# The pair stage's second layer in four column tiles of 32, the gate by Silu, row maxima by accumulation

## The chip, the cores and the metric

The kernel runs on one core of a Trainium2 chip. The metric is the device time of one execution in microseconds. Shapes in profile lines are partitions x elements; "128*32" after a matmul means 128 rows of the array by 32 of its columns.

## The reference

For 4 sequences x[b] of 512 tokens by 512 features, four blocks follow each other, each on a layer norm of the running x and each added to it: a sparse attention, a gated feed-forward, a differential attention, and the same feed-forward again. Cut to what matters here:

```python
h = einsum('bsd,fd->bsf', xn, W1)                       # 128 features
pair = relu(h[:, :, None, :] - h[:, None, :, :] + b1)   # every pair of tokens i, j
pair = relu(einsum('bijf,gf->bijg', pair, W2) + b2)     # second layer, 128 -> 64
sim = einsum('bijg,og->bijo', pair, W3)[..., 0] + b3    # one number for each pair
... # the 51 best j for each i; 32 heads of width 2 attend to these alone
h = silu(gate) * up ; out = h @ w_down                  # feed-forward, 512 -> 2048 -> 512
... 
score = softmax(attn1 - lam * attn2)                    # differential attention, 16 heads
```

The second layer of the pair stage is the largest single piece: 4 x 512 x 512 pairs, each 128 by 64.

## The kernel before

Nothing is issued where it is written. The kernel's functions record every operation as a task with its dependencies (`Plan.add`), and at the end `Plan.issue` plays the tasks through a model of the engines, with costs (`Plan.cost`), buffer counts and due times, several times over, adds a table of fixed offsets for parts of the program (`SHIFT`), and takes the order that the model ends first. The engines then get their instructions in that order, each engine in its own queue, and each queue runs in order. That is why nearly all profile lines carry the one line number L391 (the call in `issue`); the tiles' names tell the work apart. A change of a cost, a rank or an offset can therefore move any instruction of any queue.

The names: f0 to f3 is the first feed-forward of each sequence, e0 to e3 the second, b0 to b3 the differential attention; the pair stage has m, z, r and sim.

**Pair stage** (`pairs`, `pair_group`, `pair_sums`). A group is two values of i against all 512 values of j. VectorE makes m (128 features x 2 x 512) with one `min` for each i; the min form stands for the relu, and the rest is put into the bias `zb`. Each m is read as two f16 halves. TensorE multiplies by `w2s`, the second layer's weights as two f16 parts: three products for each i, into a PSUM tile z of 128 partitions, 64 output features for the first i and 64 for the second. These are matmuls with 64 output columns, so each uses half of the array's columns: column tile 0 for the first i, column tile 1 for the second. The array works on both at once if they are issued one after the other. In 80 of the 1024 groups (`ACT_TILES`) ScalarE makes m instead, in f32, and one f32 product replaces the three. ScalarE then takes z through relu into r. For every 4 groups `pair_sums` adds four matmuls with 32 columns each (four column tiles, f32) into `sim`. There are 7 PSUM buffers of the tag z, 6 of m, 10 of r, 1 of sim.

**Top-k** (`topk_tile`). For each of 16 tiles of 128 rows, VectorE finds the 51 best, GpSimd gathers their keys and values, VectorE and ScalarE (Exp) do the softmax.

**Feed-forward** (`ffn`). For 16 column blocks, 24 full-width f16 matmuls make gate and up (gu[0], gu[1]); the gate is made by ScalarE's Tanh and two VectorE passes; the product goes, as two f16 parts, into the down matmuls.

**Differential attention** (`attn_b`, `stack`). In `stack`, 64 score tiles of each sequence are made once for the softmax's maximum and sum: a VectorE `tensor_reduce` over the tile, a small VectorE product with the scale, ScalarE's Exp with an accumulated sum. Later the transposed scores pass through Exp into pt, and `products` adds four 32-column matmuls, one for each head, into av.

At the end of `hybrid_block`, `weave` puts the pair stage of sequences 1 to 3 (`main`) beside the other blocks of 0 to 2 (`side`); the rest of the blocks of 2 and 3 follow after the pairs.

Of the kernel before, what the change touches and what calls it, by code (L numbers as in the profile page):

```python
# [44 lines left out]
def _size(dt):  # L45
# [7 lines left out]
SHIFT = {  # L53
# [15 lines left out]
}  # L69
# [36 lines left out]
class Plan:  # L106
# [9 lines left out]
    DRAIN = 0.1  # L116
    BUSY = 8.0
    PERIOD = 3.41333
    LAG = {"PE": 0.2, "ACT": 0.135, "DVE": 0.12, "POOL": 0.06, "SP": 0.1}
# [8 lines left out]
    def __init__(self, nc):  # L128
        self.tasks, self.tiles, self.tags = [], {}, {}
        self.behind = ((), 0.0)  # L130
        self.pause = {}
        E = mybir.EngineType
        self.kinds = {"PE": E.PE, "ACT": E.Activation, "DVE": E.DVE, "POOL": E.Pool, "SP": E.SP}
        engs = (("PE", nc.tensor), ("ACT", nc.scalar), ("DVE", nc.vector), ("POOL", nc.gpsimd), ("SP", nc.sync))
        self.engines = [self.Engine(self, k, e) for k, e in engs]
# [57 lines left out]
    @staticmethod  # L193
    def span(ap):

        item = _size(ap.dtype)
        dims = list(ap.ap)
        lo = ap.offset
        if ap.space == DRAM:
            return 0, 1, lo * item, (lo + sum(s * (n - 1) for s, n in dims) + 1) * item  # L200
        p0 = ap.start_partition()
        lo -= p0 * dims[0][0] if lo >= dims[0][0] and dims[0][0] else 0
        return p0, p0 + ap.shape[0], lo * item, (lo + sum(s * (n - 1) for s, n in dims[1:]) + 1) * item

    def add(self, key, eng, op, a, k):
# [137 lines left out]
    def issue(self, tc, rounds=5):  # L343
# [26 lines left out]
        for r in range(rounds + 2):  # L370
# [14 lines left out]
            _, bs, _ = self.run([-e for e in end], before, nsuc, tags, True)  # L385
            rank = [-(bs[i] + tasks[i][7]) for i in range(n)]
        order = best[1]
# [7 lines left out]
def hybrid_block(ctx: ExitStack, tc: tile.TileContext, I, out):  # L395
# [64 lines left out]
    s_gu, s_d, s_a, s_p, s_w = (sc[:, i : i + 1] for i in range(5))  # L460
    c_tanh, c_down, c_exp, c_proj, c_kv, w_up, w_dn, c_nexp = (sc[:, i : i + 1] for i in range(5, 13))
    w2s = const("w2s", [128, 2, 64], F16)
# [64 lines left out]
    def prep_scales():  # L527
# [19 lines left out]
        p = [pw[:, i : i + 1] for i in range(4)]  # L547
        V.tensor_scalar(c_tanh, p[0], 2.0 ** -20, None, ALU.mult)
        V.tensor_scalar(c_down, p[0], p[0], 2.0 ** -16, ALU.mult, ALU.mult)
        V.tensor_scalar(c_down, c_down, p[1], None, ALU.mult)  # L550
# [3 lines left out]
    def prep_lambda():  # L554
# [24 lines left out]
        V.tensor_scalar(c_exp, c_exp, mx, None, ALU.mult)  # L579
        V.tensor_scalar(c_nexp, c_exp, -1.0, None, ALU.mult)  # L580


# [144 lines left out]
    def pair_group(b, it, k, g):  # L727

        hw, zb, _, _, h32, m1 = st_a[b]
        i1 = it * 128 + g * 32 + k  # L730
        m = pp.tile([128, 2, S], F32, name=f"m{b}_{i1}", tag="m", bufs=6)
        z = acct(f"z{b}_{i1}") if b == 0 and g % 2 else pzt(f"z{b}_{i1}")
        r = pp.tile([128, S], F32, name=f"r{b}_{i1}", tag="r", bufs=R_BUFS)
        if (b, it) in ACT_TILES and ACT_STEPS(k, g):

            for s in range(2):
                i = S + i1 + 16 * s
                A.activation(m[:, s, :], h32[:, 0:S], AF.Relu, scale=-1.0, bias=h32[:, i : i + 1])
                mm(z[64 * s : 64 * s + 64, :], h32[:, 2 * S :], m[:, s, :], True, True)
            bias = m1[:, 4:5]  # L740
        else:

            V.tensor_scalar(m[:, 0, :], hw[:, 0, :], hw[:, 1, i1 : i1 + 1], None, ALU.min)
            V.tensor_scalar(m[:, 1, :], hw[:, 0, :], hw[:, 1, i1 + 16 : i1 + 17], None, ALU.min)
            mv = m.bitcast(F16).rearrange("p a (n t) -> p a n t", t=2)
            for n, (w, t) in enumerate(((0, 0), (1, 1), (0, 1))):
                for s in range(2):
                    mm(z[64 * s : 64 * s + 64, :], w2s[:, w, :], mv[:, s, :, t], n == 0, n == 2)
            c = it * 64 + g * 16 + k
            bias = zb[:, c : c + 1]  # L750
        A.activation(r, z, AF.Relu, bias=bias)
        return r

    sims_open = {}

    def pair_sums(b, it, k, rr):
# [5 lines left out]
        for g in range(4):  # L762
            mm(sim[32 * g : 32 * g + 32, :], w3[:, 15 - k : 47 - k], rr[g], k == 0, k == 15)
        if k < 15:
# [132 lines left out]

    def ffn(name, X, first=False, late=False, store=lambda t: None):
        xt = yield from normed_t(name, X)
# [27 lines left out]
        for c in range(NC):  # L927
# [23 lines left out]
            t = fp.tile([128, S], F32, name=f"{name}t{c}", tag="ft", bufs=2)  # L951
            A.activation(t, gu[0], AF.Tanh, scale=c_tanh)
            V.scalar_tensor_tensor(t, t, 1.0, gu[0], ALU.add, ALU.mult)
            V.scalar_tensor_tensor(t, gu[1], 2.0 ** -35, t, ALU.mult, ALU.mult)
            ha, hb = (fp.tile([128, 2, H], F16, name=f"{name}h{p}{c}", tag="fh", bufs=FH) for p in "ab")
# [23 lines left out]
    def attn_b(name, X, first=False, late=False):  # L979
# [54 lines left out]
        def stack(g):  # L1034
# [11 lines left out]
            SP.dma_start(ks[96:98].rearrange("p h n -> p (h n)"), rows_d)  # L1046
            nm = fp.tile([128, 3, 4, 4], F32, name=f"{name}nm{g}", tag="nm", bufs=2)
            for h in range(4):
                for t in range(NT):
                    z = z_(f"{name}s{g}_{h}_{t}")  # L1050
                    mm(z, qs[0:96, h, t * 128 : (t + 1) * 128], ks[0:96, h, :], True, True)
                    V.tensor_reduce(nm[:, 0, h, t : t + 1], z, AX.X, ALU.max)
                    if True:
                        V.tensor_scalar(nm[:, 2, h, t : t + 1], nm[:, 0, h, t : t + 1], c_nexp, None, ALU.mult)
                        A.activation(z, z, AF.Exp, scale=c_exp, bias=nm[:, 2, h, t : t + 1], accum_out=nm[:, 1, h, t : t + 1])
                    yield s_cost
# [5 lines left out]
            nf = nm.rearrange("p a h t -> p (a h t)")  # L1062
            V.tensor_scalar(nf[:, 0:16], nf[:, 0:16], -(2.0 ** -11), None, ALU.mult)
            V.tensor_scalar(nf[:, 16:32], nf[:, 16:32], 2.0 ** -9, None, ALU.mult)
# [18 lines left out]
        def products(o, st, pt, l):  # L1083
            for h in range(4):
                mm(o[32 * h : 32 * h + 32, :], l(h), pt[h], st == 0, st == NT - 1)
            return 0.85

# [3 lines left out]
        for g in range(4):  # L1091
# [4 lines left out]
            for st in range(NT):  # L1096
                pt = [ppool.tile([128, S], F32, name=f"{name}pt{g}_{st}_{h}", tag=ptag, bufs=PT) for h in range(4)]
                for h in range(4):
                    z = z_(f"{name}st{g}_{st}_{h}")
                    mm(z, ks[:, h, st * 128 : (st + 1) * 128], qs[:, h, :], True, True)  # L1100
                    A.activation(pt[h], z, AF.Exp, scale=c_exp)
                    yield s_cost
                    yield next(pre, 0)
# [81 lines left out]
    def f2(b):  # L1185
        def g():
            yield from ffn(f"e{b}", X[b], late=b > 1, store=lambda t: store(b, t))
        return g
# [8 lines left out]
        lambda: start(0),  # L1197
        lambda: weave((f1(0, first=True)(), 1, 0), (phase_a(2), 0.2, 20)),
        at(0, first=True),
        lambda: weave((f2(0)(), 1, 0), (phase_a(3), 0.2, 20)),  # L1200
        lambda: start(1), f1(1), at(1), f2(1), lambda: start(2), f1(2, late=True))
    emit(weave((main, 1, 0), (side, 1.8, 120)))
# [59 lines left out]
```

## Time and profile before

| | |
|---|---|
| time, 3 runs (us) | 2619.89, 2635.37, 2633.38; median 2633.38 |
| the profiled execution's own time (us) | 2631.7 |
| its span (us) | 2629.9 |
| busy (us): TensorE, VectorE, ScalarE, GpSimd | 2556.9, 2067.3, 1516.4, 938.8 |
| matmuls and weight loads in the trace | 15044 each |
| table loads on ScalarE | 1, of 1.283 |
| first and last z of the pair stage (us from the start) | 31.9, 1876.2 |

The span is one execution as the profiler recorded it; busy time counts an instruction from its start to its modelled end, overlaps once. A matmul's duration includes the time until its result stands in PSUM, which overlaps with the next; what a matmul costs in a row is read from the distances of starts.

### The profile page before, as it was taken

The page shows a single profiled execution, that of the slowest core. Times are in us where ns is not written, and L with a number is a line of the kernel's source. Part 1 is how long each engine was busy: PE and PEld are TensorE (multiplying, and loading weights), DVE is VectorE, ACT ScalarE, POOL GpSimd, SP SyncE. Part 2 cuts the span into 40 slices and gives each one's busy share as a digit, 9 for nine tenths or more (in the row PEclk, how much of TensorE's full clock was granted, in tenths as well). Part 3 has the DMA queues.
Part 4 walks back from the last instruction along what each step waited for, and adds up shares of the span by engine and source line. Part 5 has one row for each costly group of instructions (what it writes and reads, how often), then busy time and mean ns, then how long its engine had stood idle before and what let it go on. Part 6 is the DMA issues. An engine that isn't in the chain of part 4 may idle for free.

```text
span 2629.9 us, 42770 instructions
## 1 busy us (share of the span) xinstructions
PE 2556.9 (97%) x15044; PEld 1034.6 (39%) x15044; DVE 2067.3 (79%) x5224; ACT 1516.4 (58%) x2813; POOL 938.8 (36%) x847
## 2 busy tenths in 40 slices
PE   8999999999999999999999999999999999999999
PEld 4334334343333333434433433344444444443444
DVE  8789999989999999888777899987646664574422
ACT  7998888545558984443343489753212476496211
POOL 0367677366741442673434241446143000000000
PEclk9999999999999999999999999999999999999999
DMA  6431311055761113334434421024576534532554
GB/s 203 134 116 55 101 39 51 27 173 168 228 201 38 41 53 104 118 112 149 147 103 132 137 83 41 24 77 135 181 215 193 155 95 135 179 114 89 178 157 151
DMA packets 223628, 317.79 MB, mean 121 GB/s; under 512 B 29969, under 2 KB 150865, under 8 KB 222390
## 3 DMA queue, kind: packets, MB, share of 16 engines
q1 hardware_dynamic: 197302, 261.54, 31.8%
q0 software_dynamic: 26112, 53.53, 7.1%
q8 instruction: 118, 1.93, 0.3%
q14 instruction: 96, 0.79, 0.1%
HBM read 263.43 MB, written 51.39 MB: 120 GB/s over the span
## 4 chain that ended last, share of the span: by engine, by line
PE 72%; DVE 11%; DMA 5%; issue 5%; ACT 4%; POOL 2%; another core or an unknown queue 1%; SPq 1%; DVEq 0%; ACTq 0%; POOLq 0%
PE z L391 20%; PE sim L391 7%; DVE m L391 4%; PE f1z L391 3%; PE e2z L391 3%; PE e1z L391 3%; PE e0z L391 3%; PE f3z L391 3%; PE e3z L391 2%; PE f2z L391 2%; DVE g L391 2%; POOL g L391 2%; ACT r L391 2%; PE f0z L391 1%; ACT wn L391 1%
## 5 line engine op out<-in xcount | busy, mean ns | idle before, releaser
L391 DVE TENSOR_SCALAR m<-hw 128x512 f32<-128x512 f32 x1888 | 819.7, 483 | 74.8 <-PE z L391 52.5
L391 PE MATMUL z<-m,w2s 128*64 128x512 f16 x5664 | 769.3, 393 | 19.5 <-ACT r L391 7.0
L391 ACT ACTIVATE r<-z,zb 128x512 f32<-128x512 f32 x944 | 614.2, 697 | 263.7 <-PE z L391 163.8
L391 POOL DMA_INDIRECT g<-kv,ix x432 | 473.2, 1095 | 431.5 <-DVE ix L391 313.9
L391 POOL DMA_INDIRECT g<-kv,idx x384 | 456.3, 1188 | 357.0 <-DVE idx L391 167.8
L391 PEld LDWEIGHTS <-w2s 128*64 128x64 f16 x5688 | 320.1, 108 | 531.1 <-issue 257.1
L391 PE MATMUL sim<-r,w 128*32 128x512 f32 x2048 | 329.3, 604 | 1.2 <-ACT r L391 0.8
L391 PE MATMUL z<-m,h 128*64 128x512 f32 x320 | 116.8, 599 | 1.4 <-ACT m L391 0.9
L391 ACT ACTIVATE m<-h 128x512 f32<-128x512 f32 x160 | 108.9, 731 | 13.6 <-PE z L391 11.6
L391 POOL TENSOR_SCALAR_AFFINE_SELECT sims<-sims 128x128 f32<-128x128 f32 x16 | 6.0, 378 | 285.8 <-ACT sims L391 285.7
L391 PE MATMUL f3z<-f3xt,f3w 128*128 128x512 f16 x384 | 104.6, 379 | 0.9 <-DVE f3xt L391 0.9
L391 PE MATMUL e2z<-e2xt,e2w 128*128 128x512 f16 x384 | 102.3, 379 | 0.0
L391 PEld LDWEIGHTS sim<-r,w 128*32 128x32 f32 x2048 | 50.4, 108 | 125.1 <-issue 118.5
L391 DVE TENSOR_TENSOR g<-g,sc 128x832 f32<-128x832 f32 (+3 forms) x128 | 97.7, 780 | 0.1
L391 PE MATMUL f0z<-f0xt,f0w 128*128 128x512 f16 x384 | 95.5, 380 | 1.6 <-issue 1.6
L391 PE MATMUL f2z<-f2xt,f2w 128*128 128x512 f16 x384 | 92.8, 384 | 2.2 <-DMA f2w<-wf 2.2
L391 PE MATMUL f1z<-f1xt,f1w 128*128 128x512 f16 x384 | 89.1, 385 | 4.2 <-ACT r L391 2.4
L391 PE MATMUL e3z<-e3xt,e3w 128*128 128x512 f16 x384 | 92.8, 379 | 0.1
L391 PE MATMUL e1z<-e1xt,e1w 128*128 128x512 f16 x384 | 92.6, 382 | 0.0
L391 PE MATMUL e0z<-e0xt,e0w 128*128 128x512 f16 x384 | 87.8, 379 | 0.0
L391 DVE MAX8 vm<-sims 128x8 f32<-128x512 f32 x112 | 76.3, 682 | 3.8 <-issue 2.0
L391 DVE FIND_INDEX8 ix<-vm,sims 128x8 uint32<-128x512 f32 x112 | 76.4, 682 | 0.0
(642 smaller groups left out, 3868.4 us busy)
## 6 DMA issues: line engine op xcount, KB each, us to landing
f0wr<-wf SPq DMA_DIRECT2D x48, 256.0 KB
wn<-wgu SPq DMA_DIRECT2D x32, 256.0 KB
wf<-f0w SPq DMA_DIRECT2D x16, 512.0 KB
e0w<-wf SPq DMA_DIRECT2D x16, 512.0 KB
f1w<-wf SPq DMA_DIRECT2D x16, 512.0 KB
e1w<-wf SPq DMA_DIRECT2D x16, 512.0 KB
f2w<-wf SPq DMA_DIRECT2D x16, 512.0 KB
f3w<-wf SPq DMA_DIRECT2D x16, 512.0 KB
```

The costliest lines, as they stand in the source:

```text
L391: getattr(eng, op)(*a, **k)
```

## The change

Five edits come together.

- In `pair_group` every product goes into four column tiles of 32 (`w_ = 32`): 64 output features as two matmuls of 32 columns, for each of the two i. A group has 12 f16 matmuls for 6 (or 4 f32 for 2), each with its own weight load.
- `Plan` gets `together` and `level`: the matmuls of a group share the earliest rank among them, so the model orders them side by side; and `plan.behind` makes the model treat each of a group's matmuls as ready only when both halves of m are made (for sim: when all four r are; for av: when all four pt are), with fixed pauses READY and MADE in place of the engines' general lag. These two change the order alone; the waits on the chip still follow the data.
- In `ffn`, with `silu=True` (f0, e0, f1, e1 and f2), ScalarE's Silu gives the gate, and one VectorE pass with a scalar from memory (`c_up`) multiplies by up. f3, e2 and e3 keep Tanh.
- In `stack`, one VectorE `tensor_scalar` multiplies the scores by the negative scale in place and accumulates their minimum; Exp then takes the scaled scores with a constant scale of -1. `nm` loses its third plane, and three small scalars (`c_iexp`, `c_gate`, `c_up`) are made once.
- The table `SHIFT` has new values.

```diff
+    READY, MADE = 0.185, 0.17
...
+    def together(self, n):
+        self.groups.append(range(len(self.tasks) - n, len(self.tasks)))
+
+    def level(self, rank):
+        for g in self.groups:
+            r = min(rank[i] for i in g)
+            for i in g:
+                rank[i] = r
+        return rank
...
-            rank = [-(bs[i] + tasks[i][7]) for i in range(n)]
+            rank = self.level([-(bs[i] + tasks[i][7]) for i in range(n)])
...
+        V.tensor_scalar(c_gate, p[0], 2.0 ** -19, None, ALU.mult)
+        V.tensor_scalar(c_up, ipw[:, 0:1], 2.0 ** -15, None, ALU.mult)
...
+        V.reciprocal(c_iexp, c_exp)
+        V.tensor_scalar(c_iexp, c_iexp, 2.0 ** -11, None, ALU.mult)
...
-        i1 = it * 128 + g * 32 + k
+        i1, w_ = it * 128 + g * 32 + k, 32
...
-                mm(z[64 * s : 64 * s + 64, :], h32[:, 2 * S :], m[:, s, :], True, True)
+            made = (len(plan.tasks) - 2, len(plan.tasks) - 1)
+            for s in range(2):
+                for u in range(0, 64, w_):
+                    plan.behind = (made, plan.READY)
+                    mm(z[64 * s + u : 64 * s + u + w_, :], h32[:, 2 * S + u : 2 * S + u + w_], m[:, s, :], True, True)
+            plan.together(128 // w_)
...
+            made = (len(plan.tasks) - 2, len(plan.tasks) - 1)
             for n, (w, t) in enumerate(((0, 0), (1, 1), (0, 1))):
                 for s in range(2):
-                    mm(z[64 * s : 64 * s + 64, :], w2s[:, w, :], mv[:, s, :, t], n == 0, n == 2)
+                    for u in range(0, 64, w_):
+                        plan.behind = (made, plan.MADE)
+                        mm(z[64 * s + u : 64 * s + u + w_, :], w2s[:, w, u : u + w_], mv[:, s, :, t], n == 0, n == 2)
+            plan.together(384 // w_)
...
-        return r
+        return r, len(plan.tasks) - 1
...
-            mm(sim[32 * g : 32 * g + 32, :], w3[:, 15 - k : 47 - k], rr[g], k == 0, k == 15)
+            plan.behind = (tuple(i for _, i in rr), plan.READY)
+            mm(sim[32 * g : 32 * g + 32, :], w3[:, 15 - k : 47 - k], rr[g][0], k == 0, k == 15)
+        plan.together(4)
...
+            if silu:
+                A.activation(t, gu[0], AF.Silu, scale=c_gate)
+                V.scalar_tensor_tensor(t, gu[1], c_up, t, ALU.mult, ALU.mult)
+            else:
+                A.activation(t, gu[0], AF.Tanh, scale=c_tanh)
+                V.scalar_tensor_tensor(t, t, 1.0, gu[0], ALU.add, ALU.mult)
+                V.scalar_tensor_tensor(t, gu[1], 2.0 ** -35, t, ALU.mult, ALU.mult)
...
-                    V.tensor_reduce(nm[:, 0, h, t : t + 1], z, AX.X, ALU.max)
-                    if True:
-                        V.tensor_scalar(nm[:, 2, h, t : t + 1], nm[:, 0, h, t : t + 1], c_nexp, None, ALU.mult)
-                        A.activation(z, z, AF.Exp, scale=c_exp, bias=nm[:, 2, h, t : t + 1], accum_out=nm[:, 1, h, t : t + 1])
+                    V.tensor_scalar(z, z, c_nexp, 3.0e38, ALU.mult, ALU.min, accum_out=nm[:, 0, h, t : t + 1])
+                    A.activation(z, z, AF.Exp, scale=-1.0, bias=nm[:, 0, h, t : t + 1], accum_out=nm[:, 1, h, t : t + 1])
...
-            V.tensor_scalar(nf[:, 0:16], nf[:, 0:16], -(2.0 ** -11), None, ALU.mult)
+            V.tensor_scalar(nf[:, 0:16], nf[:, 0:16], c_iexp, None, ALU.mult)
...
         def products(o, st, pt, l):
             for h in range(4):
+                plan.behind = (pt[4], plan.READY)
                 mm(o[32 * h : 32 * h + 32, :], l(h), pt[h], st == 0, st == NT - 1)
+            plan.together(4)
```

More of the change, by code (lines that the diff above doesn't have):

```diff
@@ L131, in __init__ @@
         self.pause = {}
+        self.groups = []
         E = mybir.EngineType
@@ L460, in hybrid_block @@
     s_gu, s_d, s_a, s_p, s_w = (sc[:, i : i + 1] for i in range(5))
-    c_tanh, c_down, c_exp, c_proj, c_kv, w_up, w_dn, c_nexp = (sc[:, i : i + 1] for i in range(5, 13))
+    c_tanh, c_down, c_exp, c_proj, c_kv, w_up, w_dn, c_nexp, c_gate, c_up, c_iexp = (sc[:, i : i + 1] for i in range(5, 16))
     w2s = const("w2s", [128, 2, 64], F16)
@@ L895, in hybrid_block, with ffn @@
     PARTS = ((0, 0), (0, 1), (1, 0))
-    def ffn(name, X, first=False, late=False, store=lambda t: None):
+    def ffn(name, X, first=False, late=False, silu=False, store=lambda t: None):
         xt = yield from normed_t(name, X)
@@ L951, in ffn @@
             t = fp.tile([128, S], F32, name=f"{name}t{c}", tag="ft", bufs=2)
-            A.activation(t, gu[0], AF.Tanh, scale=c_tanh)
-            V.scalar_tensor_tensor(t, t, 1.0, gu[0], ALU.add, ALU.mult)
-            V.scalar_tensor_tensor(t, gu[1], 2.0 ** -35, t, ALU.mult, ALU.mult)
+            if silu:
[5 more added lines that the diff above has]
+                V.scalar_tensor_tensor(t, gu[1], 2.0 ** -35, t, ALU.mult, ALU.mult)
             ha, hb = (fp.tile([128, 2, H], F16, name=f"{name}h{p}{c}", tag="fh", bufs=FH) for p in "ab")
@@ L1046, in stack @@
             SP.dma_start(ks[96:98].rearrange("p h n -> p (h n)"), rows_d)
-            nm = fp.tile([128, 3, 4, 4], F32, name=f"{name}nm{g}", tag="nm", bufs=2)
+            nm = fp.tile([128, 2, 4, 4], F32, name=f"{name}nm{g}", tag="nm", bufs=2)
             for h in range(4):
@@ L1096, in attn_b @@
             for st in range(NT):
-                pt = [ppool.tile([128, S], F32, name=f"{name}pt{g}_{st}_{h}", tag=ptag, bufs=PT) for h in range(4)]
+                pt = [ppool.tile([128, S], F32, name=f"{name}pt{g}_{st}_{h}", tag=ptag, bufs=PT) for h in range(4)] + [[]]
                 for h in range(4):
@@ L1101, in attn_b @@
                     A.activation(pt[h], z, AF.Exp, scale=c_exp)
+                    pt[4].append(len(plan.tasks) - 1)
                     yield s_cost
@@ L1186, in g @@
         def g():
-            yield from ffn(f"e{b}", X[b], late=b > 1, store=lambda t: store(b, t))
+            yield from ffn(f"e{b}", X[b], late=b > 1, silu=b < 2, store=lambda t: store(b, t))
         return g
@@ L1197, in hybrid_block @@
         lambda: start(0),
-        lambda: weave((f1(0, first=True)(), 1, 0), (phase_a(2), 0.2, 20)),
+        lambda: weave((f1(0, first=True, silu=True)(), 1, 0), (phase_a(2), 0.2, 20)),
         at(0, first=True),
         lambda: weave((f2(0)(), 1, 0), (phase_a(3), 0.2, 20)),
-        lambda: start(1), f1(1), at(1), f2(1), lambda: start(2), f1(2, late=True))
+        lambda: start(1), f1(1, silu=True), at(1), f2(1), lambda: start(2), f1(2, late=True, silu=True))
     emit(weave((main, 1, 0), (side, 1.8, 120)))
```

30 rows, old and new, of the table SHIFT are left out of this document.

## The prediction

> **What bounds the kernel now.** I read the page's head first, then its slices, the costliest groups, TensorE's timeline in the pair stage, the chain of waits, and last the waits of TensorE.
>
> ```profile
> span 2629.9 us, 42770 instructions
> PE 2556.9 (97%) x15044; PEld 1034.6 (39%) x15044; DVE 2067.3 (79%) x5224; ACT 1516.4 (58%) x2813; POOL 938.8 (36%) x847
> ...
> PE   8999999999999999999999999999999999999999
> ...
> DVE  8789999989999999888777899987646664574422
> ACT  7998888545558984443343489753212476496211
> ...
> PEclk9999999999999999999999999999999999999999
> ```
>
> TensorE is busy in every slice and its clock is full, so the time is TensorE's instructions plus what holds them apart. VectorE is nearly as full in the first half; it is second in line.
>
> ```profile
> L391 DVE TENSOR_SCALAR m<-hw 128x512 f32<-128x512 f32 x1888 | 819.7, 483 | 74.8 <-PE z L391 52.5
> L391 PE MATMUL z<-m,w2s 128*64 128x512 f16 x5664 | 769.3, 393 | 19.5 <-ACT r L391 7.0
> L391 ACT ACTIVATE r<-z,zb 128x512 f32<-128x512 f32 x944 | 614.2, 697 | 263.7 <-PE z L391 163.8
> ...
> L391 PE MATMUL sim<-r,w 128*32 128x512 f32 x2048 | 329.3, 604 | 1.2 <-ACT r L391 0.8
> ```
>
> VectorE's "m" and ScalarE's "r" mostly wait for TensorE's z, hardly the reverse. A matmul's 393 ns is latency, not its cost. The timeline prices it (columns: start, length, then the instructions):
>
> ```profile
> 100.34 2.42 PE L391 MATMUL z<-m,w2s 128*64 128x512 f16 x18
> ...
> 104.65 0.87 PE L391 MATMUL z<-m,w2s 128*64 128x512 f16 x6 [0.79 <-DVE m L391]
> 105.45 1.06 PE L391 MATMUL sim<-r,w 128*32 128x512 f32 x8
> 106.44 0.42 PE L391 MATMUL z<-m,w2s 128*64 128x512 f16 x2
> ```
>
> Eighteen z matmuls are nine rounds of two, side by side in the two column tiles: (2.42 - 0.39 for the last one's latency) / 9 = 0.226 us a round. Six matmuls from 104.65 are three rounds and would let the next begin at 105.33; "sim", four tiles of 32, begins at 105.45, and its own two f32 passes of 0.432 us (single starts in the trace) would end at 106.31, but z begins at 106.44. So each change of tile width costs 0.09 to 0.13 us; I take 0.09, the single starts' value (0.316 where a round is 0.226). Full-width matmuls come from the chain of waits:
>
> ```profile
> 2549.17 15.54 PE e3z L391 x72
> ```
>
> 15.54 / 72 = 0.216 us each.
>
> With these prices (0.216 full, 0.226 a narrow round, 0.432 an f32 pass, 0.09 a width change) I went once through TensorE's instructions in the order built before, each matmul starting when its own column tile is free and those ahead of it have started. That adds up to 2496 us, of which 88 are 980 width changes. The profiled execution took 2631.7 us (span 2629.9; the median of the runs is 2633.4, 0.1% more), so 136 us are waits for data, start and end. That rest grows evenly: 39 us by the first feed-forward block (at 500 us), 71 by 1020, 112 by 1890.
>
> **The change, part by part.** The same order, read from the changed program, gives these terms.
>
> 1. Width changes. z, sim and the attention's "av" now share width 32: 546 changes for 980. 434 x 0.09 = 39 us less, all on TensorE's path.
>
> 2. Half-empty rounds. Without the width changes the old order sums to 2407 us, the new one to 2379: 29 less. Most of it (20) is the 80 groups whose m ScalarE makes: each half was issued alone when its own m was there, now all four tiles are ordered together once both are. The z rounds give 10, sim and av nearly nothing. A group's first matmul now waits for the later half of m, and behind it TensorE's whole queue; the planner puts the group later by as much, and the seven z buffers hide it, unless r comes late.
>
> 3. Four tiles in a round. Arithmetic per z is unchanged: three rounds of four instead of three of two, 944 x 3 = 2832 rounds. But every round issues four weight loads and four matmuls for two and two. No row shows f16 in four tiles. Nearest below: the full-width 0.216, 0.010 under a pair's round. Above: the most matmuls that the trace starts in any 5 us are 46, 9.2 per us; at that rate four would take 0.435 us, +592 in all. Nearest by far is sim: four loads and four matmuls start 7 ns apart, and a column's next pass comes on time 0.432 us later. The last of four starts 21 ns after the first against 3 in a pair, mostly hidden in the next round. I take 0.230: +11. Bounds: -28 and +592.
>
> [...]
>
> 4. Silu. In f0, e0, f1, e1 and f2 (80 column blocks) the gate needs one VectorE pass fewer.
>
> ```profile
> L391 DVE SCALAR_TENSOR_TENSOR f0t<-f0z,f0t 128x512 f32<-128x512 f32 x16 | 10.9, 678 | 6.0 <-remote 5.8 <-PE f0z L391 0.2
> L391 DVE SCALAR_TENSOR_TENSOR f0t<-f0t,f0z 128x512 f32<-128x512 f32 x16 | 10.8, 678 | 1.9 <-ACT f0t L391 1.7 <-issue 0.2
> ...
> L391 DVE SCALAR_TENSOR_TENSOR X<-f0a,sc,X 128x512 f32<-128x512 f32 x2 | 1.4, 734 | 0.0
> L391 ACT ACT_TABLE_LOAD x1 | 1.3, 1283 | 0.8 <-PEq L1255 0.8
> ```
>
> Two passes of 678 ns become one with a scalar from memory, 734 by the X row: 0.62 us less, 50 us of VectorE in all. On the path only what TensorE waits for it counts:
>
> ```profile
> PE aop L391 <- DVE e1t L391: 4.7, 1, 4.7
> PE z L391 <- DVE f0t L391: 4.1, 2, 2.4
> ```
>
> With e0t's 1.3 that is 10 us; I take half, -5 (bounds 0 and -10). But the changed program has 23 table loads for 1: Silu and Exp alternate wherever a top-k's softmax or the attention meets a gate. 22 x 1.283 = 28 us on ScalarE, and behind each load the r that sim waits for. ScalarE is idle 42% of the time and ten r buffers stand between, so I let about a third through: +10 (bounds 0 and +28).
>
> [...]
>
> 5. Maxima. 256 times
>
> ```profile
> L391 DVE TENSOR_REDUCE b2nm<-b2s 128x1 f32<-128x512 f32 x64 | 43.5, 687 | 35.1 <-PE b2s L391 34.8
> L391 DVE TENSOR_SCALAR b2nm<-b2nm,sc 128x1 f32<-128x1 f32 x64 | 12.8, 210 | 1.0
> ```
>
> become one pass over the scores that also accumulates. Not in the trace; bounds 537 ns (xs, 128x512 in SBUF) and 810 (xnT, out of PSUM, two scalars). By the PSUM rows I take 0.75: 0.15 us less each, 38 of VectorE. The Exp after it loses its scale pointer. VectorE waits here for TensorE (34.8 of 35.1), so on the path: nothing (bounds -5, +5). If that cover went, the 38 us would be the price.
>
> 6. Everything moves: the planner gets new offsets, so every queue is reordered, SP's 1025 and POOL's 816 transfers too, none added. For the rest of 136 us I know no better value than itself; if it shrank to the idle time the page shows (2631.7 - 2556.9 = 75) it would give 61, and I keep 30 either way.
>
> Sum: 2631.7 - 39 - 29 + 11 - 5 + 10 = 2580, 2% faster. About 1% is what a measurement of this kernel can tell from no change.
>
> **The rivals.**
>
> Slower: the round of four is bound by issue. The gain of terms 1, 2 and 4 is 63 us; it is gone once a round passes 0.226 + 63 / 2832 = 0.248. At 0.270, a fifth of the way from a pair's round to the 0.435 of term 3, 2631.7 - 63 + 2832 x 0.044 = 2693. For it: twice the rate of matmuls that the trace ever holds. Against: sim's starts. Chance 0.12.
>
> No change: VectorE takes over. Up to the first feed-forward block the new order asks 412 us of TensorE; VectorE's work there, by starts (m every 0.396 us, not 0.483), is 398, where before it was 461 against 412. The two then run level, and each jitter counts. If the 49 us of that stretch are lost but for 10, and the rest stays, 2580 + 39 = 2619. For it: nines in VectorE's slices 4 to 7. Against: m's idle time ends with TensorE's z. Chance 0.14.
>
> More than forecast: order and shorter chains also thin out the waits, -30: 2550; it is inside my own case.
>
> **How the numbers follow.** Forecast 0.74, no change 0.14, slower 0.12. Low end: rounds at 0.216 (39 less than I take) and 10 from the waits: 2580 - 49, so 2531. High end: the no-change case at 2619 with all the table loads (+18) and a little of the slow round: 2645. Faster by over 1% means under 2607: 0.74; within: 0.14; slower: 0.12.
>
> **What would show it.** Right: z rounds of four start 0.226 to 0.235 us apart; TensorE's busy time falls by about 60 us; its waits stay near 75; the first feed-forward block starts near 460 us, not 500. Wrong: rounds over 0.245; "m" as the main releaser of TensorE's z before 460 us; waits of PE z for r just after table loads summing to over 30 us. A span above 2620 with rounds of 0.23 would mean that the rest of 136 us grew, term 6.

## The result: slower by 4.65%, and on another chip no change

| | before | after | ratio, 95% interval |
|---|---|---|---|
| first measurement, median of 6 runs each (us) | 2628.71 | 2746.97 | 1.0465 [1.0439, 1.0491] |
| profiled execution (us) | 2631.7 | 2746.6 | |

The forecast was 2580. The head of the page of after, some of its costliest groups, and what TensorE waited for (us in all, times, longest):

```profile
span 2744.8 us, 54646 instructions
PE 2590.4 (94%) x21028; PEld 1155.9 (42%) x21028; DVE 2014.4 (73%) x5148; ACT 1525.9 (56%) x2835; POOL 930.2 (34%) x847
...
PE   8999899789999999999999999999989899999999
...
DVE  8779988879989999678775879988455455584432
```

```profile
L403 PE MATMUL z<-m,w2s 128*32 128x512 f16 x11328 | 908.2, 396 | 63.1 <-issue 34.6
L403 DVE TENSOR_SCALAR m<-hw 128x512 f32<-128x512 f32 x1888 | 818.2, 485 | 195.0 <-PE z L403 106.9
```

```profile
PE z L403 <- issue: 35.6, 63, 1.5
PE sim L403 <- ACT r L403: 16.6, 17, 3.6
PE z L403 <- DVE m L403: 15.8, 16, 2.8
```

TensorE has 21028 matmuls for 15044, and gaps that before hardly has. VectorE, which was nearly full, is less full than before and waits for z. The longest "wait" of z is no wait: "issue" is idle time in which TensorE waited for nothing that the profile shows. One such place in TensorE's timeline (start, length, instructions, idle time before):

```profile
1925.75 1.56 PE L403 MATMUL z<-m,w2s 128*32 128x512 f16 x24
1928.18 0.42 PE L403 MATMUL z<-m,w2s 128*32 128x512 f16 x2 [0.87 <-issue]
1929.62 0.42 PE L403 MATMUL z<-m,w2s 128*32 128x512 f16 x2 [1.02 <-issue]
1931.04 1.33 PE L403 MATMUL z<-m,w2s 128*32 128x512 f16 x4 [1.00 <-issue]
1933.86 1.31 PE L403 MATMUL z<-m,w2s 128*32 128x512 f16 x4 [1.49 <-issue]
```

Twenty-four matmuls in 1.56 us, then two, two, four and four with about a microsecond between. In the single starts such a place reads load, 0.70 us, matmul, a load and a matmul at once, 0.71 us, load, 0.71 us, matmul. Call it a pause when a TensorE record (a load or a matmul) that waits for no semaphore starts 0.58 us or more after the record before it. By this count after has 86 pauses, 67 us in all, 63 of them between 0.66 and 0.74 us; before has one. (The expectations below speak of 80, by a narrower count.)

### The profile page after: what moved, and what is told of

It reads as the page before. It is cut to its first block, busy times and chain, and to the rows that moved or that the text cites. A ratio compares the mean times of both kernels' runs of the same rounds, so it can differ in the third digit from the quotient of the medians.

```text
span 2744.8 us, 54646 instructions
## 1 busy us (share of the span) xinstructions
PE 2590.4 (94%) x21028; PEld 1155.9 (42%) x21028; DVE 2014.4 (73%) x5148; ACT 1525.9 (56%) x2835; POOL 930.2 (34%) x847
## 4 chain that ended last, share of the span: by engine, by line
PE 68%; DVE 14%; ACT 5%; DMA 4%; issue 4%; POOL 2%; another core or an unknown queue 1%; SPq 0%; DVEq 0%; ACTq 0%; POOLq 0%
PE z L403 19%; PE sim L403 7%; DVE m L403 5%; PE e1z L403 3%; PE e2z L403 3%; PE f1z L403 3%; PE f3z L403 3%; PE f2z L403 3%; ACT r L403 3%; PE e0z L403 3%; DVE g L403 2%; PE e3z L403 2%; POOL g L403 2%; PE b1qk L403 1%
## 5 line engine op out<-in xcount | busy, mean ns | idle before, releaser
L403 PE MATMUL z<-m,w2s 128*32 128x512 f16 x11328 | 908.2, 396 | 63.1 <-issue 34.6
L403 POOL DMA_INDIRECT g<-kv,ix x432 | 482.5, 1117 | 466.8 <-DVE ix L403 259.5
L403 PEld LDWEIGHTS <-w2s 128*32 128x32 f16 (+1 forms) x11352 | 412.6, 95 | 491.1 <-issue 243.1
L403 POOL DMA_INDIRECT g<-kv,idx x384 | 437.3, 1139 | 458.0 <-DVE idx L403 276.3
L403 PE MATMUL sim<-r,w 128*32 128x512 f32 x2048 | 398.9, 598 | 19.7 <-ACT r L403 16.6
L403 PEld LDWEIGHTS sim<-r,w 128*32 128x32 f32 x2048 | 105.5, 108 | 132.9 <-ACT r L403 60.0
L403 PE MATMUL z<-m,h 128*32 128x512 f32 x640 | 129.6, 595 | 5.5 <-ACT m L403 3.7
L403 PE MATMUL e0z<-e0xt,e0w 128*128 128x512 f16 x384 | 95.6, 380 | 3.5 <-ACT r L403 1.9
L403 PE MATMUL e1z<-e1xt,e1w 128*128 128x512 f16 x384 | 98.3, 385 | 0.0
```

The source lines that it names most:

```text
L403: getattr(eng, op)(*a, **k)
```

## The experiments

Each set ran on one chip, the kernel before beside the rest; the chip's number is known for all but the first measurement. The times and the pauses turned out to differ between chips; chip 13 was met in one set only, and the first measurement's chip could be the same one, so whether the chip or its state at that time makes the difference is not shown. "A chip with pauses" is short for either.

**First set, chip 7: the narrow tiles alone, the wide tiles in the new order, Tanh for Silu, twice the instructions without narrow tiles.** Before took 2585.2 us here. In x1 and x4 the planned order of before is kept, and a product is split only as it is given to the engine.

```diff
 x1: before, each z matmul as two of 32 columns
+ for u in (0, 32):  z[64*s+u : 64*s+u+32, :], w2s[:, w, u:u+32], mv[:, s, :, t]
 x2: after's order, each pair of 32-column matmuls as one of 64
+ if u == 0:         z[64*s : 64*s+64, :],     w2s[:, w, :],      mv[:, s, :, t]
 x3: after
-                A.activation(t, gu[0], AF.Silu, scale=c_gate)
+                A.activation(t, gu[0], AF.Tanh, scale=c_gate)
 x4: before, each f16 z matmul as two halves of j
+ for v in (0, 256): z[64*s : 64*s+64, v:v+256], w2s[:, w, :], mv[:, s, v:v+256, t]
```

x3 computes another gate; the work is the same, without table loads.

> The kernel before, same order of all queues, but each 64-column z matmul is issued as two of 32 columns one after the other (the planner does not know). By the prices of before the order sums to 2457 us on TensorE (2496 before), so with the old rest of 136 us: 2593. Theory A, TensorE runs out of instructions when twice as many are issued (the 0.70 us pauses without a semaphore, 80 of them in the trace after): pauses like those appear, 60 us or more, and the time is 2640 to 2700. Theory B, the new order and its pauses are at fault: no pauses, about 2593. Theory C, the table loads: about 2593.

> The changed kernel in its own order of all queues, but each two 32-column z matmuls of one half are issued as one of 64 columns at the place of the first. The order was not made for that: it has 1189 width changes and sums to 2589 us on TensorE (2428 as it was). Theory A (instruction supply): the 0.70 us pauses are gone, and the rest over the sum falls from 319 us to 150 to 230, so 2740 to 2820. Theory B (order): the rest stays at 319 or more, 2900 and over. Theory C (table loads): the rest falls by nothing either, 2900.

> The changed kernel with Tanh in Silu's place, all else and every queue's order kept: the gate's value is wrong, and the 22 additional table loads are gone. Theory C (table loads): 2747 falls to 2690 or less. Theories A and B: the loads' own 28 us at most, a third of it by the forecast, so 2725 to 2745.

> The kernel before in its own order, two column tiles of 64, but each f16 z matmul of 512 columns is issued as two of 256 with a weight load each, alternating between the two column tiles: as many TensorE instructions as after the change, the same array time (the order sums to 2502 us, 2496 before), no four tiles. Theory A (instruction supply): pauses of 0.70 us without a semaphore, and 2690 to 2760. Theory D, four column tiles are slow in themselves: 2630 to 2645, no pauses. Theories B and C: the same 2630 to 2645.

| | us | ratio to before there | pauses |
|---|---|---|---|
| x1, narrow tiles alone | 2565.8 | 0.9938 [0.9916, 0.9961] | 0 |
| x2, new order in wide tiles | 2717.5 | 1.0520 [1.0499, 1.0542] | 1 |
| x3, Tanh for Silu | 2581.2 | 0.9993 [0.9980, 1.0006] | 2 |
| x4, instructions doubled, wide tiles | 2598.7 | 1.0051 [1.0033, 1.0069] | 0 |

None of these has the changed kernel's pauses. x2 is slow for another reason: the new order with two tiles has 1189 width changes and adds up to 2589 us. The times expected for x1, x2 and x4 all missed: they were worked out from the first measurement, and before itself took some 45 us less here. x3 fell where theory C had it, as if Silu's tables cost 160 us, but only until the next set had the changed kernel itself on that chip.

**Second set, chip 7: the two kernels again, and the changed kernel with two wide tiles (`w_ = 64`, planned anew).**

> The changed kernel itself, nothing edited, beside the kernel before on the same chip as the other experiments if it is the same. In those the kernel before took 2585 us, not 2629, and no kernel showed 0.70 us pauses. Theory C (the table loads): 2690 or more, as Tanh in Silu's place gave 2581. Theory E, the pauses come and go with the chip or the run, not with the kernel's text: 2590 to 2615, with fewer than 20 pauses.

> The kernel before, for its profile on this chip. Theory E: the rest over the sum of 2496 us is smaller by some 45 us here than in the first profile, spread evenly over the pair stage. If it is the same 136, the runs before differ by chance.

> The changed kernel with w_ = 64 and a plan made for it: two column tiles, groups side by side, Silu and maxima kept. Its order sums to 2445 us (882 width changes), 51 less than before. Theory A (instruction supply) and E: no pauses, rest as in the kernel before on this chip (89) and a third of the loads: 2540 to 2560. Theory C (table loads): 2640 or more. Theory B (order): 2600 or more.

The unchanged text of after took 2583.7 us, ratio 1.0001 [0.9990, 1.0011]; before, one profiled run, 2585.5; two tiles 2572.9, 0.9958 [0.9944, 0.9972], over the 2540 to 2560 expected. So x3 beside r1 says that the 22 added table loads (23 of 1.283 us in the first trace of after, 1 in before) cost some 2.5 us on this chip, which is within the noise of the two ratios, and that the 4.65% are not in the program alone. r1's 2583.7, with 2 pauses, lies a little under what theory E gave (2590 to 2615). Here are the same pages' heads for after and then before on chip 7:

```profile
span 2581.5 us, 54646 instructions
PE 2497.0 (97%) x21028; PEld 1145.7 (44%) x21028; DVE 2006.0 (78%) x5148; ACT 1522.9 (59%) x2835; POOL 962.3 (37%) x847
```

```profile
span 2583.7 us, 42770 instructions
PE 2540.2 (98%) x15044; PEld 1030.0 (40%) x15044; DVE 2064.5 (80%) x5224; ACT 1519.0 (59%) x2813; POOL 945.8 (37%) x847
```

Both kernels gain on chip 7, before 46 us, after 163, and of the 86 pauses of after 2 are left.

**Third set, chip 13: VectorE made lighter, in three kernels, and after once more.** In each top-k tile three in-place passes are left out (the striking-out of the eight best, the products with q and with the softmax); TensorE's program and all orders stay.

```diff
                 V.match_replace(s, vm[:, sl], s, -3.0e38)
+                plan.parts[len(plan.tasks) - 1] = []
...  the same after the two products of g
```

> The changed kernel with its order kept, but with three in-place VectorE passes of every top-k tile left out: the match_replace that strikes out the best eight, the product of the gathered keys with q, and the product of the gathered values with the softmax (some 50 us of VectorE before the first feed-forward block, some 190 in all). TensorE's program is the same, 2419 us by the sum. Theory V (where the first measurement's slowdown is absent, the gain of terms 1 to 3 is eaten because VectorE is the next bound of the pair stage): the rest over the sum falls from 156 to 100 or less, so 2500 to 2530 us; the first feed-forward block starts at 445 us or before, not at 479. Theory S (TensorE's own supply of instructions or its order eats it, VectorE doesn't matter): 2565 to 2585 us, the block still near 475.

> The kernel before with the same three VectorE passes of every top-k tile left out, order kept; TensorE's program is the same, 2486 us by the sum. Theory V: here TensorE is the bound, its rest was 90 already, so 2560 to 2575 us, a fall of 10 to 25, far less than the same relief brings in the changed kernel. Theory S: much the same fall in both kernels, under 20 us.

> The order of before with each 64-column product of the pair stage issued as two of 32 (2566 us so far, sum 2447), and the same three VectorE passes of every top-k tile left out. Theory V: 2500 to 2540 us, the full 39 us of the width changes below the lightened kernel before. Theory S: 2550 to 2565.

> The changed kernel once more, unchanged. Theory E (the 0.7 us pauses and the 118 us come with a chip or its state, not with the program): on the chip that gave 2584 it is within 2575 to 2590 again, with under five pauses; on another chip it may be anything from 2580 to 2760. If the program alone made them, 2747.

| chip 13, before 2641.5 us | us | ratio to before | pauses |
|---|---|---|---|
| after | 2751.3 | 1.0417 [1.0382, 1.0451] | 85 |
| after, VectorE lighter | 2760.0 | 1.0445 [1.0420, 1.0469] | 99 |
| before, VectorE lighter | 2634.3 | 0.9962 [0.9936, 0.9988] | 2 |
| x1, VectorE lighter | 2756.9 | 1.0431 [1.0401, 1.0460] | 144 |

The times expected for the three lighter kernels missed under either theory, because the set met a chip of the other kind; r3's allowed for that. (The sums named there, 2419, 2486 and 2447, are 9 or 10 us under those used elsewhere; nothing here rests on them.) But the set says more than it was made for. The changed kernel is slow again, with 85 pauses. Lighter VectorE work brings the changed kernel nothing, and before 0.4%. And the last two rows differ only in how the pair stage's products are issued: splitting them into narrow tiles, in before's own order, with Tanh and the old maxima, costs 2756.9 / 2634.3 = 1.047, as much as the whole change. The same edit won 0.6% on chip 7. In TensorE's waits, the longest row of x1, then that of before and its row for the same wait, both lighter:

```profile
PE z L393 <- issue: 49.3, 110, 1.3
```

```profile
PE z L393 <- ACT r L393: 7.6, 6, 1.8
...
PE z L393 <- issue: 2.5, 6, 0.9
```

49.3 us of idle time without a wait against 2.5.

**Fourth set, chip 0, and three single runs on chips 15, 0 and 4, to settle whether the number of instructions or the narrow tile does it.** m_rates is TensorE alone with constant operands; r4 and h are x1, x4 and e1 again; y_mixed splits into narrow tiles in even blocks of rows and into halves in odd ones.

> Not the layer: TensorE alone, with constant operands, 600 rounds each of (a) pairs of 64x512, (b) fours of 32x512, (c) pairs of 64 in halves of 256 columns, (d) fours of 32 in halves, then 120 loads of 256 KB on SP beside (e) fours and (f) pairs. A round is 512 columns for each pair of i. Instructions (loads and matmuls) per round: 4, 8, 8, 16. Theory A (TensorE's instructions come at a limited rate, which differs between chips): (a) 0.226 us everywhere; (d) far above 0.226 us on any chip, which gives the rate in instructions per us; on a chip that has the pauses also (b) and (c) above 0.24. Theory M (the sustained rate is enough, and only the meeting with other work, such as transfers, starves it): (b), (c) at 0.226 to 0.23 without transfers, (e) above 0.24. If all but (d) stay at 0.226 on a chip with pauses, the supply fails only in the mix of the real kernel.

> The order of before, each 64-column product of the pair stage issued as two of 32; nothing else. On chip 7 it took 2566 (0.994 of before). Theory A: on a chip where the changed kernel takes 2750, this alone takes 2720 to 2770, ratio 1.03 to 1.05, with 50 to 150 pauses of 0.7 us. Rival (the other edits, Silu, maxima or the planner's order, do the harm): within 1% of before there too. On chip 7 again: 0.994.

> The order of before, two tiles of 64 columns kept, each product in two halves of 256 columns: as many instructions as the changed kernel, but no narrow tile. On chip 7 1.005 of before. Theory A: on a chip with pauses 1.02 to 1.05, since the count of instructions is what matters. Rival (four narrow tiles are slow there, not the count): under 1.01. On chip 7 again: 1.005.

> The changed kernel with w_ = 64, planned anew: Silu, maxima, groups and offsets stay, only the four narrow tiles go (sum 2445 us). On chip 7 0.996 of before. Theory A: 0.985 to 1.0 on every chip, the faster of the two kernels there; under five pauses. Rival (the other edits do the harm on a chip with pauses): 1.02 or more there.

> The order of before, two tiles of 64 columns kept, each product in two halves of 256 columns: as many TensorE instructions as the changed kernel, no narrow tile. On chips without pauses 1.005 of before. Theory A (the number of instructions): on a chip where before takes some 2630 us and the changed kernel 2750, this takes 1.02 to 1.05, with tens of pauses of 0.7 us. Theory N (only the four narrow tiles starve there): under 1.01 and under ten pauses.

> The changed kernel with w_ = 64, planned anew: Silu, maxima, groups and offsets stay, only the four narrow tiles go. On chips without pauses 0.996 of before. On a chip where before takes some 2630 us and the changed kernel 2750: theory A or N (the harm there is the narrow tiles' doubled instructions) 0.985 to 1.0 of before with under five pauses; the rival (the other edits do part of the harm) 1.01 or more.

> The order of before; in the even blocks of 128 rows each product of the pair stage is issued as two of 32 columns, in the odd blocks as two halves of 256 columns of j: the same number of instructions in both. On a chip without pauses 0.998 to 1.003 of before, no pauses in either kind of block. On a chip with pauses: theory A (the number of instructions) pauses and slow stretches in both kinds of block alike, ratio 1.03 or more; theory N (the narrow tiles) nine tenths of the pauses in the even blocks, ratio 1.01 to 1.03.

| | chip | us | ratio to before there | pauses |
|---|---|---|---|---|
| r4_x1 | 0 | 2570.5 | 0.9946 [0.9927, 0.9966] | 1 |
| r4_halves | 0 | 2594.9 | 1.0048 [1.0032, 1.0064] | 0 |
| r4_two_tiles | 0 | 2573.9 | 0.9971 [0.9960, 0.9983] | 2 |
| h5_halves | 15 | 2595.8 | 1.0050 [1.0033, 1.0067] | 1 |
| h6_two_tiles | 0 | 2574.3 | 0.9966 [0.9948, 0.9985] | 2 |
| y_mixed | 4 | 2618.8 | 1.0147 [1.0126, 1.0168] | 3 |

None of these met a chip with the pauses, so the question stays open. y_mixed missed its expectation (0.998 to 1.003) too: in its odd blocks both halves of a product follow each other on one column tile, where x4 alternates between the two, so by the order rounds stay half empty (an estimate from the order; measured are the 1.0147 on chip 4 for x4's 1.0051 on chip 7); it says nothing on the pauses. m_rates gives the price of a round by itself, 600 rounds to a group:

```profile
L55 PE MATMUL fourh<-m,w 128*32 128x256 f16 x4800 | 133.0, 273 | 1.2 <-issue 0.9
L55 PE MATMUL halves<-m,w 128*64 128x256 f16 x2400 | 131.2, 273 | 0.0
L55 PE MATMUL fours_dma<-m,w 128*32 128x512 f16 x2400 | 129.8, 379 | 0.0
L55 PE MATMUL pairs_dma<-m,w 128*64 128x512 f16 x1200 | 129.7, 379 | 0.0
L55 PE MATMUL fours<-m,w 128*32 128x512 f16 x2400 | 129.7, 379 | 0.0
```

129.7 / 600 = 0.216 us for a round of four as for a pair, and no more beside transfers (247 GB/s through `fours_dma`; they had ended before `pairs_dma`). In halves of narrow tiles, where sixteen loads and matmuls go into a round, 0.222. So chip 0 ran 9600 loads and matmuls in 134 us, 72 per us; the changed kernel asks for at most 31 over any 50 us. The slow rounds that theories A and M expected did not come, but on a chip without pauses.

## Why the prediction was wrong

**The prices held (terms 1, 2 and 3).** Where nothing stops TensorE, rounds of four start 0.227 us apart in after (the median of 1204 rounds; 103.015, 103.241 and 103.468 us are three starts in a row), where a pair's round has a median of 0.226 in before on chip 7, and m_rates has 0.216 for both, no price for the four tiles. The slower rival, a round of 0.270, is out. The sum of the new order by the prices is 2496 - 39 - 29 = 2428 us.

**Term 6 failed, and it failed twice.** "For the rest of 136 us I know no better value than itself" was the step: the rest was carried over from before to after, give or take 30. Profiled time less sum:

| | before | after |
|---|---|---|
| first measurement | 2631.7 - 2496 = 136 | 2746.6 - 2428 = 319 |
| chip 7 | 2585.5 - 2496 = 90 | 2583.3 - 2428 = 155 |

The same kernel before has a rest of 136 us in one place and 90 in the other, so 46 of the 136 were the chip's, not the program's.

*The chips with pauses.* The prediction named this outcome: a span above 2620 with rounds of 0.23. The place was right, its size, 30, was not: the rest grew by 183. Compare after with itself, the first measurement against chip 7, by the distances between consecutive TensorE records (counted from the trace). Of 163 us, 65 are in distances of 0.58 us or more before a record that waits for nothing (86 of them, against 2). Another 39 are in distances of 0.33 to 0.58 us, also without a wait. 69 are in distances of 0.33 us or more before a record that waits for a semaphore, -9 in the short ones. The third part may follow on the first two, as in this place: from 284.16 to 285.33 us TensorE starts nothing and waits for nothing, ScalarE is idle until it begins an m at 285.40, and TensorE's next loads wait 0.66 us for that m. The clock takes a share as well: its mean of 0.984 over the span, for 0.992 on chip 7, is 44 us of full clock lost against 21, so 23 of the 163 us at most, spread over these parts.

So TensorE stops where it waits for nothing that the profile shows, and the narrow tiles alone bring it on (v_x1_light against v_before_light). That its instructions come late is the author's guess; no view shows them arrive. No cap on the mean rate shows: at its densest, after has 30.8 TensorE instructions per us over 50 us in the first measurement and on chip 7 alike. It is single stoppages. One DMA queue, q8, keeps step with TensorE's records: one packet of 16 KB for every 256 of them (165 for 42210 in after, 118 for 30240 in before). Whether TensorE ever waits for these packets no run settles: in the first measurement they take a median of 0.99 us in after and 1.01 in before, and half of the pauses of after come 139 records or more after the last packet began.

Two more things can be read from the traces. The pauses belong to places in the program: 71 of the 86 of the first measurement come back in r3, on chip 13, within 20 TensorE records of the same place. And they go with GpSimd's gathers: in the 0.7 us before a pause, the gathers' queue (q0) had a packet in flight for 85% of the pauses in after, 91% in r3 and 85% in v_x1_light, against 46, 48 and 42% before z's loads and matmuls at large. No run varied the gathers, so their part stays untested. Open are: what stops TensorE; what differs between the chips; and whether it takes the number of instructions or the narrow tile.

The profile of before had a sign of it, in rows that the prediction did not use. ScalarE's waits of before in the first measurement, VectorE's, and then ScalarE's largest such row on chip 7:

```profile
ACT r L391 <- issue: 23.1, 18, 6.2
```

```profile
DVE f2t L391 <- issue: 15.7, 9, 3.1
```

```profile
ACT f2t L391 <- issue: 2.5, 1, 2.5
```

All such rows together are 91 us for ScalarE and 43 for VectorE in the first measurement, 8 and 4 on chip 7; on chip 13, in v_before_light, 90 and 62. (GpSimd's are some 200 us everywhere and tell nothing.) On the first chip these engines stood idle without a wait in before already, for up to 6 us, off the path. Only TensorE, with 15044 matmuls, had all but none (2.4 us). The edit that doubled the pair stage's matmuls brought such idle time onto the path. In the prediction term 3 weighed the doubled instructions only as a price for each round, not as something that can make TensorE stop.

*The chips without pauses.* Here the 68 us of the sum were also given back: the rest grew by 65, and the result is no change, the middle rival. Busy time from 200 to 480 us, the pair stage before the first feed-forward block, in after and then before on chip 7 (after the length come TensorE, its loads, VectorE, ScalarE, GpSimd, the granted clock, the DMA engines' share and GB/s):

```profile
200.00:480.00 280.00, 256.75 (x3160) 134.00 (x3155) 270.16 (x679) 229.73 (x378) 192.78 (x160) 0.98 0.21 58
```

```profile
200.00:480.00 280.00, 278.25 (x1898) 105.86 (x1890) 270.34 (x657) 231.68 (x382) 186.58 (x156) 1.00 0.21 59
```

VectorE is 96% busy in both; in before TensorE is 99% busy beside it, in after 92%. "m" is now what z waits for:

```profile
PE z L403 <- DVE m L403: 20.5, 20, 3.1
```

where before has, on the same chip,

```profile
PE z L391 <- DVE m L391: 3.3, 5, 1.1
```

Against the sum, after loses 47 us in this stretch, before 9: 38 of the 65. The other 27 are not placed; the clock, with a mean of 0.992 for 0.997, can make up 13 of the 65 at most. The first feed-forward block starts at 479 us, not at the 460 predicted (before 490). That is the rival's sign, "m as the main releaser"; it was argued, and got 0.14, so that the middle outcome came on chip 7 was foreseen, but not expected. That VectorE is the cause is read from these rows and not shown by an experiment: the runs with lighter VectorE work met the other kind of chip, where they changed nothing, as there VectorE has time to spare:

```profile
200.00:480.00 280.00, 257.33 (x2975) 122.78 (x2977) 244.32 (x600) 221.16 (x364) 172.83 (x147) 0.99 0.18 55
```

(after, first measurement: TensorE 92% and VectorE 87%, neither full.)

**Terms 4 and 5.** The table loads, taken at +10, cost some 2.5 us on chip 7 (x3 against r1, within the noise); the gain taken for the lighter gate, -5, was not measured by itself. The maxima pass was priced right, at 0.754 us for 0.75, but a record was missed that the accumulation brings:

```profile
L403 DVE TENSOR_SCALAR_CACHE_REDUCE b2s<-b2s,sc 128x512 f32<-128x512 f32 x64 | 47.2, 754 | 17.8 <-PE b2s L403 17.6
...
L403 DVE DVE_READ_ACCUMULATOR b2s<-b2s,sc 128x1 f32 x64 | 9.1, 142 | 0.0
```

0.754 + 0.142 is 0.896 us, the 0.897 of the two passes it replaces: the 38 us taken off VectorE do not exist, and its busy time fell by 53 us instead of 88. On the path it was priced at nothing, so the forecast didn't suffer.

**Beside the forecast.** On chips 7 and 0 the changed kernel with two wide tiles (e1, r4_two_tiles, h6) takes 2573 to 2574 us, 0.3 to 0.4% under before and under after's 2584 on chip 7; x1 takes 2566 to 2571, but its lighter form was 4.3% over before on chip 13. Two wide tiles weren't met by a chip with pauses.

## What to carry to other kernels

Read the "issue" rows of every engine, the idle ones too: here VectorE's and ScalarE's told the chips with pauses from the others before the change was made, and an edit that doubles the matmuls of the engine on the path brought such idle time onto the path. A sum of prices says what the bound engine asks for; when it falls by as little as here (2496 to 2428, 2.7%), ask what the second engine has left in that stretch (here 4%) before any of it is counted as gain. And before a large difference is explained, run both kernels again on another chip.

## What was not expected of the hardware

- One program, two kinds of chip, or of its state: after takes 2747 and 2751 us on two measurements and 2584 on chip 7, before 2629 and 2642 against 2580 to 2585 on chips 0, 4, 7 and 15. The granted clock, 0.984 against 0.992 for after, makes up 23 of the 163 us at most.
- TensorE stops for some 0.70 us on a record without a wait, several times in a row with few instructions between: 86 pauses in after, 144 in v_x1_light, at most 3 in any run of the kernel on chips 0, 4, 7 and 15. They come at the same places of the program in two measurements, and mostly while GpSimd's gathers are in flight.
- Each accumulating VectorE pass over the scores in after leaves a second record behind it, of 136 to 142 ns.
